# Cross attention of a four-layer decoder: queries masked at the eviction, and the attends of two chunks of heads issued together

## The chip, the cores and the metric

The kernel runs on one core of a Trainium2 chip. A core has a matrix engine (TensorE, in the profile PE, with its weight loads as PEld), a vector engine (VectorE, DVE), a scalar engine (ScalarE, ACT), GpSimd (POOL) and a queue for transfers (SyncE, SP). Each engine works through its own instructions in order, and semaphores tie them together. Matrix products land in PSUM, a small memory of eight banks; DVE or ACT must evict them to the working memory (SBUF). The metric is the device time of one execution in microseconds (us), and the times given are medians of several runs.

## The reference

The model is a decoder of four layers (L0 to L3), each with a self-attention, a cross-attention and a feed-forward part, on 8 sequences of 112 tokens with 256 features; the cross attentions look at 8 contexts of 375 positions with 128 features. Three of the four cross attentions run through the function that is changed here. The one of the last layer stands for them:

```python
Q = (x @ Wq.T).reshape(B, xN, NUM_HEADS, HEAD_DIM)          # 16 heads of 16
KV = (z @ Wkv.T).reshape(B, zN, 2, NUM_HEADS, HEAD_DIM)
attn = jnp.einsum('bqhd,bkhd->bhqk', Q, K) * SCALE          # SCALE = 16 ** -0.5
attn = jax.nn.softmax(attn, axis=-1)
O = jnp.einsum('bhqk,bkhd->bqhd', attn, V).reshape(B, xN, DIM)
return O @ Wo.T
```

That of layer 1 has the same shape and biases on queries, keys, values and output. That of layer 2 (called a2 here, the second of two attentions in its part) has 16 heads of 32 features and no such biases.

## The kernel before

`cross` (from L1260) computes one cross attention. `l1_xattn` calls it for layer 1 (named l1x, with heads of 16), `a2_attend` for layer 2 (a2, heads of 32) and `l3_xattn` for layer 3 (l3x, heads of 16). The heads of 16 are the dense case (`dense = hd == 16`).

The 16 heads are taken as four chunks c of four heads j. One step is a pair (b, c) of a batch b and a chunk c, so a stage has 32 steps. For one step:

- `score(b, c)`: for each of four heads a product of 32 rows on TensorE, queries by keys, into one of four PSUM buffers `sc` of 112 tokens by 375 positions. The four heads lie in four groups of 32 rows of the matrix engine and run side by side.
- `exponent(b, c)`: for each head the maximum over the positions on DVE (L1338, tile `xnm`), then the exponential on ACT (L1342 in the dense case, L1344 in a2, where it also gathers the sum), tile `xe`.
- `turn(b, c, j)`: three transposes on TensorE (L1351) that bring the positions onto the partitions, into one of two PSUM buffers `tr`, and one eviction to the tile `xeT`: heads 0 and 2 on DVE (L1359), heads 1 and 3 on ACT (L1357).
- `attend(b, c)`: the weights by the values, 12 products of 32 columns each (four heads by three pieces of 125 positions, L1367), gathered in the one PSUM buffer `av` of the batch. After the last chunk ACT copies `av` to the tile `xoT` (L1377).

The profile counts two records for each product of 32-bit numbers, one for each transpose, so an attend is 24 records and a step's scores are 8.

Around these stand `key` and `value` (keys and values of the next batch), `query` (queries, by halves of four batches; half 0 ahead of the loop, half 1 within it), `summed` and `divide` (sums of the weights, their reciprocals, and the division) and `result` (the output projection, and its addition to the stream). Keys, values, queries, sums and results all pass through one PSUM buffer, `mm` (the pool `ps1` has one buffer for each name), so whoever writes it next waits until it has been evicted.

In the dense case a row group of 32 rows holds two heads of 16 in the keys. The weights of the queries are laid out by `_halves` (512 columns, half of them zero), so that the query tile `qT` has four chunks in each of which only one of the two heads of a row group is not zero. `score` takes chunk c of `qT` with chunk c // 2 of the keys.

The loop over the steps runs with a schedule written out by hand (L1414): TensorE, DVE and ACT take their instructions in the order of the code. In one step n = (b, c): `turn` of heads 0 and 1; a key chunk of the next batch, or at odd c in the dense case `summed` (c=1) or `divide` (c=3) of the batch before; `turn` of head 2; `score` of step n+1; `turn` of head 3; `exponent` of step n+1; `value` of the next batch (c < 3); at c=3 of the first two batches two chunks of `query` for half 1; at c=3 `result` of the batch before; `attend` of step n. What stands ahead of the loop is ordered by the scheduler of the language.

Steps with c=0 and c=2 are called even below, those with c=1 and c=3 odd.

The weights are packed on the host into blobs, which SyncE loads in order through a ring of eight buffers (`w<-in_w`, and `w<-in_wl` for the last layer). Small columns (biases, scales) lie in one tile, `vec`.

Of the kernel before, what the change touches and what calls it, by code (L numbers as in the profile page):

```python
# [26 lines left out]
AF = mybir.ActivationFunctionType  # L27
ALU = mybir.AluOpType
# [4 lines left out]
P = 128  # L33
# [13 lines left out]
def _fm(w):  # L47

    k, n = w.shape
    return w.reshape(k // P, P, n).transpose(1, 0, 2).reshape(P, -1)  # L50


def _col(v):

    return v.reshape(-1, P).T
# [17 lines left out]
_SLOTS = [8 * (n // 2) + 2 * j + n % 2 for n in range(4) for j in range(4)]  # L73
# [4 lines left out]
    return w.reshape(-1, 16, 16)[:, _SLOTS].reshape(w.shape)  # L78


def _halves(w):

    out = np.zeros((w.shape[0], 4, 4, 2, 16), w.dtype)
    a = w.reshape(-1, 16, 16)[:, _SLOTS].reshape(-1, 4, 4, 16)
    for n in range(4):
        out[:, n, :, n % 2] = a[:, n]
    return out.reshape(-1, 512)

_SHIFT = np.tile(np.arange(32) == 16, 16).astype(np.float32)
# [33 lines left out]
def _weights(inp):  # L125
    def g(layer):
        return lambda name: inp[f"{layer}_{name}"]

    a, xa, f = g("L0_attn"), g("L0_xattn"), g("L0_ffn")
# [33 lines left out]
    a, xa, f = g("L1_attn"), g("L1_xattn"), g("L1_ffn")  # L163
# [9 lines left out]
            ("l1a_bo", _row(a("bo"))),  # L173
        ],
        [
            ("l1x_wq", _fm(_halves(xa("Wq")))),
            ("l1x_wk", xa("Wk")),
            ("l1x_wv", _slots(xa("Wv"))),
            ("l1x_bv", _row(_slots(xa("bv")[None])[0])),
# [7 lines left out]
    for j in range(3):  # L187
        cols = slice(512 * j, 512 * j + 512)
        blobs.append([(f"l1f_gate{j}", _fm(gate[:, cols])), (f"l1f_up{j}", _fm(up[:, cols]))])
    for j in range(2):  # L190
# [1 line left out]
    v1 = [  # L192
        ("l1a_bq", _col(_spread(a("bq")[None])[0])),
        ("l1a_bk", _col(_spread(a("bk")[None])[0] + _SHIFT)),
        ("l1x_bq", _col(_halves(xa("bq")[None])[0])),
        ("l1x_bk", _col(xa("bk"))),
    ]

    a, xa, f = g("L2_attn"), g("L2_xattn"), g("L2_ffn")
# [39 lines left out]
    for pf in ("a1", "a2"):  # L239
        for n in ("lnx_g", "lnx_b", "lny_g", "lny_b", "ln3_g", "ln3_b", "li2_b"):  # L240
            v2.append((f"{pf}_{n}", _col(xa(f"{pf}_{n}"))))

    a, xa, f = g("L3_attn"), g("L3_xattn"), g("L3_ffn")
# [7 lines left out]
    ]  # L251
    last = [
        [
            ("l3x_wq", _fm(_halves(xa("Wq").T))),
            ("l3x_wk", wkv[:, :D]),
            ("l3x_wv", _slots(wkv[:, D:])),
        ],
# [5 lines left out]
    v3 = [  # L263
        ("l3f_s_in", np.broadcast_to(f("s_in")[None, :], (P, 1))),
        ("l3f_s_in_down", np.broadcast_to(f("s_in_down")[None, :], (P, 1))),
    ]
    return (blobs, ternary, last), own, ints, raw, v0 + v1 + v2 + v3


# [110 lines left out]
class _Kernel:  # L380
# [879 lines left out]
    def cross(self, name, cT, qsrc, wq, wk, wv, wo, hd, scale, finish, ctx, bq=None, bk=None, bv=None):  # L1260
# [14 lines left out]
        nc, tc = self.nc, self.tc  # L1275
# [37 lines left out]
        def query(half, c):  # L1313
            cols = slice(half * HT, (half + 1) * HT)
            pm = self.t(ps1, [P, 512], "mm")[:, :HT]
            self.mm(pm, [(wq[:, k, c * P : (c + 1) * P], self.xnT[:, k, cols]) for k in range(2)])
            if bq is None and half == 0:
                nc.scalar.activation(qT[:, c, cols], pm, AF.Copy, scale=scale)
            elif bq is None:
                nc.vector.tensor_scalar(qT[:, c, cols], pm, scale, None, ALU.mult)  # L1320
            else:
                nc.vector.tensor_scalar(qT[:, c, cols], pm, self.v(bq, c), scale, ALU.add, ALU.mult)
# [39 lines left out]
        def attend(b, c):  # L1362
            if c == 0:
                avs[b] = self.t(ps1, [P, 512], "av")
            for i in range(NCH):
                for j in range(4):
                    nc.tensor.matmul(  # L1367
                        avs[b][32 * j : 32 * j + 32, c * S : (c + 1) * S],
                        values[b % 2][:CH, i, 4 * c + j, :],
                        eTs[b, c, j][:, i, :],  # L1370
                        start=i == 0,
                        stop=i == NCH - 1,
                        skip_group_check=True,
                    )
            if c == 3:
                oTs[b] = self.t(work, [P, 4, S], "xoT")
                nc.scalar.copy(oTs[b], avs.pop(b)[:, : 4 * S].rearrange("p (c s) -> p c s", c=4))  # L1377
# [29 lines left out]
        for i in range(NCH):  # L1407
            value(0, i)
        qsrc(ps, 0)
        for c in range(4):  # L1410
            query(0, c)
        qsrc(ps, 1)
        steps = [(b, c) for b in range(NB) for c in range(4)]
        with tc.manual_schedule(engines={ET.PE, ET.DVE, ET.Activation}):  # L1414
            score(0, 0)
            exponent(0, 0)
            for n, (b, c) in enumerate(steps):
                turn(b, c, 0)
                turn(b, c, 1)

                if not dense or c % 2 == 0:
                    if b + 1 < NB:
                        key(b + 1, c * nk // 4)
                elif b > 0:
                    (summed, divide)[c // 2](b - 1)
                turn(b, c, 2)
                if n + 1 < len(steps):
                    score(*steps[n + 1])
                turn(b, c, 3)
                if n + 1 < len(steps):  # L1430
                    exponent(*steps[n + 1])
                if c < 3 and b + 1 < NB:
                    value(b + 1, c)
                if c == 3 and b < 2:
                    query(1, 2 * b)
                    query(1, 2 * b + 1)
                if not dense and b > 0 and c == 1:
                    divide(b - 1)
                if b > 0 and c == 3:
                    result(b - 1)  # L1440
                attend(b, c)
                if not dense and c == 3:
                    summed(b)
            if dense:
                summed(NB - 1)
            divide(NB - 1)
            result(NB - 1)
# [1230 lines left out]
```

## Time and profile before

| | |
|---|---|
| median of 3 runs | 2171.72 us (2168.49 to 2174.79) |
| the profiled execution | 2168.82 us, its span 2167.0 us |
| stage l1x, 706 to 900 | 194 us, PE busy 179.82, DVE 129.57, ACT 100.13 |
| stage a2, 1370 to 1570 | 200 us, PE busy 186.44, DVE 137.16, ACT 121.71 |
| stage l3x, 1871 to 2057 | 186 us, PE busy 173.78, DVE 124.03, ACT 101.60 |
| one full batch, l1x (772.59 to 792.08) | 19.49 us |
| one full batch, a2 (1462.26 to 1482.83) | 20.57 us |
| one query chunk on PE | 1.70 us |
| one attend, start to start of what follows | 0.71 to 0.90 us |
| granted TensorE clock, mean of the span | 0.946 of full speed |

The rows shown further on come from three kinds of view. The page gives the busy time of each engine. A timeline gives, for each merged group of instructions, its start, its duration, the engine, the line of the kernel, the operation, the tile written and those read, the shape of the output and the inputs, the count, and in square brackets the idle time of that engine before it with what ended it. The view of busy time by stretch gives for each stretch its length, then busy time and instruction count of PE, PEld, DVE, ACT and POOL, then the granted clock, the share of the transfer engines and their GB/s. A busy PE is not a PE at its peak: matmuls overlap in its pipeline.

### The profile page before, as it was taken

How to read it: one execution, taken by the hardware profiler on the slowest of the kernel's cores; microseconds unless marked ns; L12 is line 12 of the kernel's file. 1: busy time of each engine (PE TensorE's matmuls, PEld its weight loads, DVE VectorE, ACT ScalarE, POOL GpSimd, SP SyncE). 2: the span in 40 equal slices, each digit the busy share in tenths (PEclk: the TensorE clock that was granted, in tenths of full speed). 3: DMA queues.
4: the chain of work that ended last, by engine and by line, in shares of the span. 5: the costliest groups of instructions: out<-in, count | busy, mean ns of one | idle time of the engine just before them, and what ended most of it. 6: DMA issues, size and time to landing. Idle time of an engine off the chain costs nothing. (4 is left out here: it accounts for less than half of the span.)

```text
span 2167.0 us, 45439 instructions
## 1 busy us (share of the span) xinstructions
PE 1938.5 (89%) x17912; PEld 1244.4 (57%) x17912; DVE 1386.8 (64%) x3905; ACT 869.0 (40%) x2420; POOL 281.9 (13%) x480
## 2 busy tenths in 40 slices
PE   7999999898898899899899989899998997899844
PEld 3545544465666566545566455556667886566623
DVE  5666666686655677553566676567624866667688
ACT  2444444562212456452033223466525322356532
POOL 1111111001302100000001342100003530100000
PEclk9999999998899999999999999999999997999956
DMA  5000001103000000223101010000022210000000
GB/s 208 3 3 3 3 22 39 33 21 107 1 1 16 21 2 2 79 89 135 40 1 59 1 42 8 1 2 2 1 78 72 98 39 26 1 2 2 2 0 17
DMA packets 11486, 69.20 MB, mean 32 GB/s; under 512 B 1290, under 2 KB 3082, under 8 KB 4874
## 3 DMA queue, kind: packets, MB, share of 16 engines
q1 hardware_dynamic: 9684, 54.69, 7.0%
q0 software_dynamic: 1584, 11.54, 1.5%
q8 instruction: 145, 2.38, 0.4%
q14 instruction: 73, 0.60, 0.1%
HBM read 65.30 MB, written 0.92 MB: 31 GB/s over the span
## 5 line engine op out<-in xcount | busy, mean ns | idle before, releaser
L727 PE MATMUL g<-w,hT 128*32 128x256 f32 x3552 | 236.7, 384 | 1.8 <-DVE hT L757 1.5
L1338 DVE TENSOR_REDUCE xnm<-sc 112x1 f32<-112x375 f32 x384 | 184.6, 541 | 40.0 <-PE sc L444 39.4
L1351 PEld LDWEIGHTS tr<-cst,xe 112*125 112x125 f32 x1152 | 151.5, 188 | 94.6 <-issue 38.1
L1351 PE MATMUL tr<-cst,xe 112*125 112x112 f32 x1152 | 192.9, 289 | 6.8 <-DVE xeT L1359 4.2
L727 PEld LDWEIGHTS g<-w,hT 128*32 128x32 f32 x3552 | 93.2, 109 | 121.8 <-DVE hT L757 83.0
L1357 ACT COPY xeT<-tr 125x336 f32<-125x336 f32 x192 | 85.4, 445 | 158.1 <-PE tr L1351 158.1
L444 PE MATMUL mm<-xnT,w 128*128 128x448 f32 x316 | 136.0, 572 | 9.4 <-DVE qT L1320 2.9
L1359 DVE COPY xeT<-tr 125x336 f32<-125x336 f32 x192 | 97.3, 507 | 68.6 <-PE tr L1351 61.8
L690 PE MATMUL g<-xw,cst 128*32 128x256 f32 x1792 | 137.9, 379 | 0.0
L1342 ACT ACTIVATE xe<-sc,xnm 112x375 f32<-112x375 f32 x256 | 126.6, 582 | 7.3 <-DVE xnm L1338 7.3
L753 ACT ACTIVATE th<-cell 128x64 f32<-128x64 f32 x224 | 57.5, 257 | 144.3 <-DVE cell L749 141.9
L444 PE MATMUL mm<-w,hT 128*112 128x256 f32 x448 | 103.4, 392 | 0.0
L740 ACT ACTIVATE sg<-g 128x192 f32<-128x192 f32 x224 | 74.1, 331 | 67.3 <-PE g L727 45.6
L444 PEld LDWEIGHTS mm<-xnT,w 128*128 128x128 f32 x316 | 60.0, 200 | 67.9 <-issue 44.2
L576 POOL TENSOR_TENSOR hTlo<-xnT,hThi 128x448 fp32r<-128x448 f32 x60 | 74.9, 1256 | 160.8 <-issue 82.7
L444 PE MATMUL mm<-hThi,w 128*128 128x448 f32 x256 | 95.2, 372 | 0.0
L444 PE MATMUL mm<-hTlo,w 128*128 128x448 f32 x256 | 94.7, 370 | 0.0
L444 PEld LDWEIGHTS mm<-w,hT 128*112 128x112 f32 x448 | 81.7, 184 | 21.7 <-issue 3.5
L758 POOL COPY hs<-hT 128x16 f32<-128x16 f32 x224 | 51.8, 231 | 318.4 <-DVE hT L757 318.4
L755 DVE TENSOR_TENSOR h<-sg,th 128x64 f32<-128x64 f32 x224 | 50.5, 226 | 63.9 <-ACT th L753 63.8
L444 PE MATMUL sc<-xkT,qT 32*112 32x375 f32 x768 | 89.8, 519 | 0.0
L1367 PE MATMUL av<-xeT,xv 125*32 125x112 f32 x2304 | 86.4, 266 | 2.1 <-ACT xeT L1357 2.1
(482 smaller groups left out, 3961.9 us busy)
## 6 DMA issues: line engine op xcount, KB each, us to landing
w<-in_w SPq DMA_DIRECT2D x22, 1024.0 KB, 5.0
t<-in_wt SPq DMA_DIRECT2D x11, 1024.0 KB, 4.9
w<-in_wt POOLq DMA_DIRECT2D x11, 1024.0 KB, 5.4
raw<-in_wq SPq DMA_DIRECT2D x3, 1024.0 KB, 5.2
cx<-in_ctx SPq DMA_DIRECT2D x2, 1500.0 KB
wi<-in_wint SPq DMA_DIRECT2D x3, 768.0 KB, 5.6
w<-in_w SPq DMA_DIRECT2D x2, 896.0 KB, 10.7
w<-in_w SPq DMA_DIRECT2D x2, 768.0 KB, 4.1
```

Source lines behind the costliest of these rows:

```text
L444: self.nc.tensor.matmul(out, lhsT, rhs, start=i == 0, stop=i == len(pairs) - 1)
L576: nc.gpsimd.tensor_tensor(dst[1], src, dst[0].bitcast(F32), ALU.subtract)
L690: nc.tensor.matmul(g[32 * j : 32 * j + 32, :], pick[:, t % 16, :], xw[:, l, t // 16, 256 * j : 256 * j + 256], start=True, stop=t == 0, sk ...
L727: nc.tensor.matmul(g[32 * j : 32 * j + 32, :], hT[l][:, c, :], whh[l][:, c, 256 * j : 256 * j + 256], start=False, stop=c == 1, skip_group ...
L740: nc.scalar.activation(sg[:, :192], g[:, :192], AF.Sigmoid)
L753: nc.scalar.activation(th, cell[l], AF.Tanh)
L1338: nc.vector.tensor_reduce(nm, sc, AX.X, ALU.max, negate=True)
L1342: nc.scalar.activation(e, sc, AF.Exp, bias=nm)
L1351: nc.tensor.transpose(tp[:CH, i * S : (i + 1) * S], e[:, i * CH : (i + 1) * CH], self.ident[:S, :S])
L1357: nc.scalar.copy(eT, src)
L1359: nc.vector.tensor_copy(eT, src)
L1367: nc.tensor.matmul(avs[b][32 * j : 32 * j + 32, c * S : (c + 1) * S], values[b % 2][:CH, i, 4 * c + j, :], eTs[b, c, j][:, i, :], start=i ...
```

## The change

There are two parts.

The queries of the dense case are no longer spread over four half-empty chunks. Their weights have 256 columns, so `query` makes two chunks, and each is evicted twice into `qT`: once multiplied by a column that is 0.25 in the rows of even heads and 0 in those of odd heads, once by the opposite column (`turn0` and `turn1`, two new columns in `vec`; as l1x's query bias shrinks from four columns to two, the tile keeps its width). In l1x both evictions are on DVE, which adds the bias as well; in l3x the first is on DVE and the second on ACT. `qT` holds the same numbers as before, and `score` is unchanged.

The attends of an even and the following odd step are issued together at the end of the odd step. The place of the queries for half 1 moves: in the dense case one of two chunks at c=3 of each of the first two batches, in a2 one of four chunks at c=1 and c=3 of them.

```diff
-def _halves(w):
-
-    out = np.zeros((w.shape[0], 4, 4, 2, 16), w.dtype)
-    a = w.reshape(-1, 16, 16)[:, _SLOTS].reshape(-1, 4, 4, 16)
-    for n in range(4):
-        out[:, n, :, n % 2] = a[:, n]
-    return out.reshape(-1, 512)
-
+_EVEN = [(np.arange(P) // 16 % 2 == p).astype(np.float32)[:, None] for p in range(2)]
...
-            ("l1x_wq", _fm(_halves(xa("Wq")))),
+            ("l1x_wq", _fm(xa("Wq"))),
...
-        ("l1x_bq", _col(_halves(xa("bq")[None])[0])),
+        ("l1x_bq", _col(xa("bq"))),
...
-            ("l3x_wq", _fm(_halves(xa("Wq").T))),
+            ("l3x_wq", _fm(xa("Wq").T)),
...
+    v3 += [(f"turn{p}", np.float32(0.25) * _EVEN[p]) for p in range(2)]
...
             self.mm(pm, [(wq[:, k, c * P : (c + 1) * P], self.xnT[:, k, cols]) for k in range(2)])
-            if bq is None and half == 0:
+            if dense:
+                for p in range(2):
+                    out, even = qT[:, 2 * c + p, cols], self.v(f"turn{p}")
+                    if bq is not None:
+                        nc.vector.tensor_scalar(out, pm, self.v(bq, c), even, ALU.add, ALU.mult)
+                    elif p:
+                        nc.scalar.activation(out, pm, AF.Copy, scale=even)
+                    else:
+                        nc.vector.tensor_scalar(out, pm, even, None, ALU.mult)
+            elif bq is None and half == 0:
...
         qsrc(ps, 0)
-        for c in range(4):
+        for c in range(nk):
             query(0, c)
...
-                if c == 3 and b < 2:
-                    query(1, 2 * b)
-                    query(1, 2 * b + 1)
+                if dense and c == 3 and b < 2:
+                    query(1, b)
+                elif not dense and c % 2 and b < 2:
+                    query(1, 2 * b + c // 2)
                 if not dense and b > 0 and c == 1:
                     divide(b - 1)
                 if b > 0 and c == 3:
                     result(b - 1)
-                attend(b, c)
+                if c % 2:
+                    attend(b, c - 1)
+                    attend(b, c)
```

## The prediction

> **What bounds the kernel now.** I read the page first, then busy time by stretch for the three stages that run `cross`, then the timeline of one steady batch, first of TensorE (PE) alone, then of all engines. The page makes PE the busiest engine:
>
> ```profile
> PE 1938.5 (89%) x17912; PEld 1244.4 (57%) x17912; DVE 1386.8 (64%) x3905; ACT 869.0 (40%) x2420; POOL 281.9 (13%) x480
> ```
>
> The stages take 194 us (l1x, from 706), 200 us (a2, from 1370) and 186 us (l3x, from 1871); PE is busy 93% of each. That is an average over steps with two different limits. All engines, third batch of l1x, tail of step c=0 and head of c=1:
>
> ```profile
> 775.37 1.91 DVE L1338 TENSOR_REDUCE xnm<-sc 112x1 f32<-112x375 f32 x4 [0.37 <-PE sc L444]
> 775.53 0.30 PEld L444 LDWEIGHTS mm<-w,ctxT 128*125 128x125 f32 x2
> 775.63 0.61 PE L444 MATMUL mm<-w,ctxT 128*125 128x256 f32 x2
> 775.88 0.44 ACT L1357 COPY xeT<-tr 125x336 f32<-125x336 f32 x1 [1.13 <-PE tr L1351]
> 776.17 0.73 PEld L1367 LDWEIGHTS av<-xeT,xv 125*32 125x32 f32 x24 [0.33 <-issue]
> 776.17 0.97 PE L1367 MATMUL av<-xeT,xv 125*32 125x112 f32 x24
> 776.22 1.97 ACT L1342 ACTIVATE xe<-sc,xnm 112x375 f32<-112x375 f32 x4
> 777.07 0.73 PEld L1351 LDWEIGHTS tr<-cst,xe 112*125 112x125 f32 x6 [0.17 <-issue]
> 777.07 0.91 PE L1351 MATMUL tr<-cst,xe 112*125 112x112 f32 x6
> 777.20 0.42 DVE L1309 TENSOR_TENSOR xv<-mm,w 125x256 f32<-125x256 f32 x1
> 777.69 0.51 DVE L1359 COPY xeT<-tr 125x336 f32<-125x336 f32 x1
> ```
>
> The scores of the next step started at 774.38. Their first exponential is done at 776.22 + 0.58 = 776.80; the next transposes start at 777.07. So the attend, 0.90 us from 776.17 to 777.07, is what PE does while it would otherwise wait. Behind it one chain runs without a gap: four maxima, value copy (xv), copy of the turned weights (xeT), and only then the third transposes (two PSUM buffers `tr`). The last batch shows that chain alone, having no keys and values to make (l3x, PE alone):
>
> ```profile
> 2032.56 0.90 PE L444 MATMUL sc<-xkT,qT 32*112 32x375 f32 x8
> ...
> 2034.56 0.76 PE L1367 MATMUL av<-xeT,xv 125*32 125x112 f32 x18 [0.26 <-ACT xeT L1357]
> ...
> 2037.20 0.90 PE L444 MATMUL sc<-xkT,qT 32*112 32x375 f32 x8
> ```
>
> Score to score is 4.64 us, exactly that of c=0 in a full batch (774.38 to 779.02), though 0.54 us of PE work (value) is missing. Taking PE work from an even step therefore buys almost nothing; adding it to an odd step, which is full, costs its length.
>
> **Part 1, queries.** Half 1, second batch of l1x, PE alone:
>
> ```profile
> 764.95 1.68 PE L444 MATMUL mm<-xnT,w 128*128 128x448 f32 x4
> 767.41 1.77 PE L444 MATMUL mm<-xnT,w 128*128 128x448 f32 x4 [0.78 <-DVE qT L1322]
> 769.96 1.98 PE L444 MATMUL mm<-w,xoT 128*112 128x256 f32 x8 [0.78 <-DVE qT L1322]
> ```
>
> A chunk is 1.70 us of PE, and whoever takes the single PSUM buffer `mm` next waits 0.72 to 0.78 us for its eviction. The l1x and l3x stages lose 4 of 8 chunks each; evictions stay 8, two to a chunk. An eviction with a pointer scalar took 0.684 us on DVE (L1322), with an immediate 0.625 (L1320), on ACT 0.544 (L1318). No row has two pointers, or ACT with a pointer scale; I take 0.68 and 0.55, and as upper ends 0.9 (the sum of a 0.68 pass and a 0.2 small DVE row) and the 0.653 of another ACT row with a pointer bias (L810).
> - l1x, first batch: two chunks and a gap, 743.13 to 747.29 = 4.16, become 1.70, the attends not needing `mm`: -2.46. Second batch: the result starts at 769.96; now 764.95 + 1.70, then two DVE evictions, about 768.07: -1.89.
> - l3x, first batch 1903.25 to 1907.35 becomes 1.70: -2.40. Second: DVE and ACT evict one each, but ACT first finishes its exponentials (1925.61 + 1.97), so the result moves from 1929.91 to about 1928.17: -1.74.
> - Before the loop, l1x: the order becomes query, two scores, query, two scores, transposes. With evictions at 719.11 to 720.45, scores at 719.86, second query at 720.7, its evictions to 723.85, the last two maxima to 724.9 and the first copy of turned weights to 725.4, the scores of step (0,1) start at 725.9, not 728.63: -2.7. The l3x analog lands at 1885.2, not 1888.76: -3.5.
> - a2 keeps four chunks but spreads them over c=1 and c=3. At c=1 the value has just taken `mm`, and DVE copies it only after its four maxima (about 1404.07, PE done at 1402.85). The query must wait 1.29 us, and both attends are queued behind it on PE. Before: 4.10 + 4.89 = 8.99 us in two batches; after: twice (1.29 + 1.70), 1.70, and 1.70 + 0.72 = 10.1: +1.1.
> Sum -14.7 + 1.1 = -13.6. Two weight loads on SP's queue shrink by 256 KB each; the queue keeps its order, POOL's nothing changes, and DMA is at 0 to 2% share in these stages: 0 (if a load were late the stage's first key would wait for it, and it waits for DVE).
>
> **Part 2, pairs of attends.** PE alone, an attend after a result:
>
> ```profile
> 791.36 0.78 PE L1367 MATMUL av<-xeT,xv 125*32 125x112 f32 x24
> 792.08 0.91 PE L1351 MATMUL tr<-cst,xe 112*125 112x112 f32 x6
> ```
>
> It holds PE 0.72 us. Its six groups of four start 0.1 apart (0.097 from the second on), the last at 791.87, so some 0.14 of the 0.72 is the change to the transposes. A second attend directly behind costs 6 x 0.097 = 0.58 more if its groups run on, 0.72 at worst (as if alone); I take 0.58, the groups being of one form. After a value the attend takes 0.90, because 0.18 is a wait for the fourth copy on ACT; in a pair that wait is gone.
> - Dense stages, by batch. Even steps: transposes start at 776.86, not 777.07, but behind them the value's buffer and the xeT copy hold; c=0 gains 0.09, c=2 gains 0.12 (its divide waits for that copy, before as after). c=1: 0.90 becomes 0.72 + 0.58, +0.40. c=3: +0.58. Sum +0.77, times 7 full batches = 5.4. Last batch +0.25. In one batch the next stage's normalisation stands differently among DVE's maxima (four rows of 0.41 before the copy instead of three): +0.3. Each stage +5.95, both +11.9.
> - a2: no wait on ACT there (attend 0.71). Even steps -0.16 each. c=1 +0.16: the second transposes wait there for the divide anyway (1472.88, where 1472.09 + 0.37 = 1472.46 would do), and 0.42 of the second attend falls into that. c=3 +0.58. Sum +0.42 by 6 = 2.5, first batch (no divide) +0.8, last +0.3, normalisation +0.3: +3.9.
> Unseen are PE's even-step waits. Bounds: an even step can't go below 4.44, the shortest score-to-score step of the last batch, against 4.64, 4.80 and 4.72 now; that is 0.11, 0.24 and 0.12 a step more than I take, 7 us over 22 batches. A second attend at 0.72 in 48 pairs is 6.7 worse. I stay with the replay, nearest to the 4.64 of the last batch.
>
> **Sum.** -13.6 + 11.9 + 3.9 = +2.2 us on the profiled 2168.82 (span 2167.0 and 1.8 around it): 2171.0. The median, 2171.72, lies 2.9 higher: 2174. I count within 0.3% (6.5 us) as no change, about what a measurement of this kernel can tell: 2165.2 to 2178.2.
>
> **Weighed against the skill.** The Trainium skill, "Perfetto Trace Analysis", section on the most-contended engine, says to optimise the busiest engine first. The last batch's 4.64 speaks against it here; by the rule, with PE work setting all steps, the sum would be about 30 us of gain.
>
> One pair of rows warns of the clock (busy time by stretch; the column after POOL's is the granted clock):
>
> ```profile
> 836.00:839.00 3.00, 2.56 (x24) 1.82 (x22) 2.70 (x8) 1.00 (x3) 0.62 (x1) 1.00 0.01 3
> 839.00:843.00 4.00, 4.00 (x38) 2.87 (x35) 2.28 (x6) 2.31 (x5) 0.00 (x0) 0.57 0.00 0
> ```
>
> After 0.44 us of short PE waits the clock fell to half for 3.4 us, and that step took 5.86 instead of 4.48: 1.4 us. The change adds a wait of some 0.7 us to every even step. The last batch of each stage, with 0.6 us of waits in each step, kept 1.00, so I count no more such events. The skill's "TensorE: Matmul & The Clock Gate", section "A second HAM failure mode: psum-queue depth-cycling", says that frequent micro-idles make the clock oscillate; by it every pair could lose 1.4 us, some 60 in all, while no run here shows that.
>
> **Rivals.**
> - *The clock drops (slower).* For: the two rows. Against: the last batches. At 1.4 us an event, four more make it slower by over 0.3%; one in each of 22 batches gives +31, so 2205. Chance 0.10.
> - *Pairing at full price (slower).* Second attend 0.72 and no even step shorter: +6.7 and, for the lost 0.21 (dense) and 0.32 (a2) a batch, +5.4, so +14.3: 2186. Chance 0.12.
> - *The query saving is hidden (doesn't do what it says).* Double evictions hold `mm` longer and DVE's later copies slip; half of 14.7 goes: +9.6, 2181. Against: DVE idles 1.8 to 2.1 us in these steps. Chance 0.06.
> - *PE sets the even step (faster).* For: 89% busy and the 0.90 attend. Against: the 4.64. At the floor of 4.44 it gives 2167, still no change; with both attends' 0.90 (a2 0.71) taken out of every batch's even steps about 2142. It decides where each of the 44 even steps shortens by 0.2 us more than I take. Chance 0.12.
> - My forecast, 0.60; its own range is 2167 to 2181.
>
> **Numbers.** Faster 0.12, same 0.60, slower 0.10 + 0.12 + 0.06 = 0.28. The range 2163 to 2187 takes in both ends of the pairing and the two nearer slow rivals, and leaves out most of the clock's case and half of the fast one.
>
> **What would show it.** PE should wait 0.6 to 0.7 us for ACT's xe before the transposes of odd steps in l1x; score to score should read about 4.55, 4.88, 4.68, 6.15 in a full batch where it was 4.64, 4.48, 4.80, 5.57; two attends together 1.30. Step (0,1)'s scores should come 2.7 (l1x) and 3.5 us (l3x) sooner after the first query; in a2 a query should wait about 1.3 us for the value's copy. Wrong if even steps shorten by over 0.3 us, or the granted clock shows new stretches of 0.50.

## The result, and the profile after

The changed kernel takes 2177.4 us in the median of nine executions (2175.3 to 2190.0), beside 2170.2 us for the kernel before on the same chip: 1.0043 times as long, with a 95% interval from 1.0030 to 1.0055. A second set, given as an experiment below, says 1.0040 (1.0026 to 1.0054). So the change makes the kernel slower, by +7 us between medians and by 9 us by the ratio. I had put 2174.0 us and +2.2 us, and 0.28 on slower. Of all executions below, one of e10 took 2533.08 us at a mean granted clock of 0.723; it is left out of that ratio.

The profiled execution of the changed kernel is the slowest of the nine, at 2189.99 us. Its steady batch on TensorE alone, third batch of l1x (columns as in the timelines of the prediction; L1354 are the transposes, L1370 the attends, L438 the helper of all products):

```profile
772.71 0.90 PE L438 MATMUL sc<-xkT,qT 32*112 32x375 f32 x8
...
774.49 1.36 PE L1370 MATMUL av<-xeT,xv 125*32 125x112 f32 x48
775.78 0.91 PE L1354 MATMUL tr<-cst,xe 112*125 112x112 f32 x6
...
777.58 0.90 PE L438 MATMUL sc<-xkT,qT 32*112 32x375 f32 x8
...
780.05 1.04 PE L1354 MATMUL tr<-cst,xe 112*125 112x112 f32 x6 [0.61 <-ACT xe L1345]
...
782.27 0.90 PE L438 MATMUL sc<-xkT,qT 32*112 32x375 f32 x8
...
785.34 1.36 PE L1370 MATMUL av<-xeT,xv 125*32 125x112 f32 x48
...
788.43 0.90 PE L438 MATMUL sc<-xkT,qT 32*112 32x375 f32 x8
```

From these scores on, score to score reads 4.87, 4.69 and 6.16 us, and 4.58 into the first of them (from 768.13); I had put 4.55, 4.88, 4.68 and 6.15. The two attends hold PE from 774.49 to 775.78, 1.29 us; I had put 1.30. Before the transposes of the odd step PE waits 0.61 us for ACT's `xe`; I had put 0.6 to 0.7. A batch takes 20.30 us instead of 19.49, +0.81 where the prediction said +0.77. The step-by-step replay is right to some hundredths of a microsecond.

What isn't in the replay stands in the last batch of the same stage. TensorE alone, then busy time by stretch (length, then busy time and instruction count of PE, PEld, DVE, ACT and POOL, the granted clock, the share of the transfer engines, GB/s):

```profile
872.08 0.90 PE L438 MATMUL sc<-xkT,qT 32*112 32x375 f32 x8
...
874.55 1.04 PE L1354 MATMUL tr<-cst,xe 112*125 112x112 f32 x6 [1.06 <-ACT xe L1345]
...
876.80 1.61 PE L438 MATMUL sc<-xkT,qT 32*112 32x375 f32 x8
...
879.24 2.47 PE L1370 MATMUL av<-xeT,xv 125*32 125x112 f32 x48
...
883.78 0.90 PE L438 MATMUL sc<-xkT,qT 32*112 32x375 f32 x8
```

```profile
876.50:878.50 2.00, 2.00 (x11) 0.73 (x11) 0.67 (x3) 0.00 (x0) 0.61 (x1) 0.50 0.00 0
878.50:880.50 2.00, 2.00 (x31) 1.80 (x35) 1.91 (x4) 1.10 (x3) 0.00 (x0) 0.50 0.00 0
880.50:882.50 2.00, 2.00 (x32) 1.67 (x25) 0.00 (x0) 1.20 (x3) 0.00 (x0) 0.50 0.00 0
```

The even step has no attend, key or value left here: PE waits 1.06 us for `xe`, until 874.55. By 876.50 the granted clock stands at 0.50. The scores take 1.61 us instead of 0.90, the pair of attends 2.47 instead of 1.36, and the step from 876.80 to 883.78 takes 6.98 us; it took 4.44 before. PE's rows look busy, 2.00 us of 2.00, which is what a half clock looks like in a timeline: no idle time, only longer instructions. The stretch that the kernel before had in the sixth batch of this stage (839 to 843 in the prediction's rows) is there too, from 835.45: its step takes 6.48 us instead of 4.87.

In l3x this execution loses the clock in the middle batches too, in three in a row and then in the last; one of them, by stretch:

```profile
2026.00:2028.00 2.00, 1.77 (x13) 0.83 (x13) 1.23 (x3) 0.70 (x3) 0.00 (x0) 1.00 0.01 4
2028.00:2030.00 2.00, 1.46 (x11) 1.24 (x11) 1.93 (x5) 2.00 (x5) 0.00 (x0) 1.00 0.00 0
2030.00:2032.00 2.00, 2.00 (x13) 1.77 (x16) 0.64 (x2) 0.21 (x1) 0.61 (x1) 0.53 0.03 8
2032.00:2034.00 2.00, 2.00 (x12) 0.95 (x5) 0.92 (x3) 0.00 (x0) 0.00 (x0) 0.50 0.00 0
2034.00:2036.00 2.00, 2.00 (x31) 1.35 (x33) 1.45 (x4) 1.89 (x5) 0.00 (x0) 0.50 0.00 0
```

The 0.77 us wait of PE before `xe` lies between 2027.78 and 2028.55, and the clock falls at 2030. From its first to its last scores l3x takes 172.94 us here. In a second execution of the same kernel (below) it takes 160.72 us, without one such stretch.

### The profile page after: what moved, and what is told of

Same layout as the page of the kernel before. It is cut to its first block, busy times and chain, and to the rows that moved or that the text cites. A ratio compares the mean times of both kernels' runs of the same rounds, so it can differ in the third digit from the quotient of the medians.

```text
span 2188.2 us, 45327 instructions
## 1 busy us (share of the span) xinstructions
PE 1937.3 (89%) x17880; PEld 1251.1 (57%) x17880; DVE 1386.2 (63%) x3905; ACT 869.5 (40%) x2420; POOL 280.3 (13%) x480
## 5 line engine op out<-in xcount | busy, mean ns | idle before, releaser
L1354 PEld LDWEIGHTS tr<-cst,xe 112*125 112x125 f32 x1152 | 160.1, 194 | 143.7 <-ACT xe L1345 39.3
L1354 PE MATMUL tr<-cst,xe 112*125 112x112 f32 x1152 | 207.6, 301 | 32.4 <-ACT xe L1345 22.4
L438 PE MATMUL mm<-xnT,w 128*128 128x448 f32 x284 | 122.7, 576 | 6.4 <-DVE xv L1301 2.4
L438 PE MATMUL mm<-w,hT 128*112 128x256 f32 x448 | 103.0, 391 | 0.0
L438 PE MATMUL mm<-hThi,w 128*128 128x448 f32 x256 | 94.6, 370 | 0.0
L438 PE MATMUL mm<-hTlo,w 128*128 128x448 f32 x256 | 94.2, 368 | 0.0
L438 PEld LDWEIGHTS mm<-w,hT 128*112 128x112 f32 x448 | 81.4, 183 | 21.8 <-issue 3.7
L438 PE MATMUL sc<-xkT,qT 32*112 32x375 f32 x768 | 92.5, 538 | 1.5 <-DVE qT L1319 0.9
L438 PEld LDWEIGHTS mm<-xnT,w 128*128 128x128 f32 x284 | 55.0, 203 | 57.4 <-issue 41.6
L684 PEld LDWEIGHTS g<-xw,cst 128*32 128x32 f32 x1792 | 58.7, 110 | 38.7 <-issue 0.3
```

The lines of the kernel that those rows point to most:

```text
L438: self.nc.tensor.matmul(out, lhsT, rhs, start=i == 0, stop=i == len(pairs) - 1)
L684: nc.tensor.matmul(g[32 * j : 32 * j + 32, :], pick[:, t % 16, :], xw[:, l, t // 16, 256 * j : 256 * j + 256], start=True, stop=t == 0, sk ...
L1354: nc.tensor.transpose(tp[:CH, i * S : (i + 1) * S], e[:, i * CH : (i + 1) * CH], self.ident[:S, :S])
```

## The experiments

Two theories stood against each other. Theory A: the replay is right at an unchanged clock, and the rest is clock lost behind the waits that pairing exposes. Theory B: a pair costs more on the path than I replayed, at full clock. The runs are called e1 to e11, as in what was expected of them.

### The two parts alone

Queries alone (e1): the attends stay one in each step, and a2 keeps its query chunks at c=3.

```diff
-                elif not dense and c % 2 and b < 2:
-                    query(1, 2 * b + c // 2)
...
+                elif not dense and c == 3 and b < 2:
+                    query(1, 2 * b)
+                    query(1, 2 * b + 1)
...
-                if c % 2:
-                    attend(b, c - 1)
-                    attend(b, c)
+                attend(b, c)
```

> The query part of the change alone, dense stages; each step keeps its own attend, and a2's queries stay two chunks at c=3. The replay of the prediction says -14.7 us (l1x -7.05, l3x -7.64) against the kernel before, about 2155 to 2156, with the half-clock stretches of the kernel before and no new ones, since no PE wait of over 0.3 us is added in a steady step. The rival 'the query saving is hidden' says about half of it: -7, 2163.

Measured: 2158.58 us, 0.9934 (0.9916 to 0.9953), so -12.8 us between medians and -14.3 by the ratio. From the first key product to the last projection l1x takes 182.60 us instead of 189.60, -7.00, and l3x 176.37 instead of 183.79, -7.42; the replay had -7.05 and -7.64. What did differ by a little was the evictions: with two pointers DVE takes 0.739 us (I took 0.68), ACT with a pointer scale 0.638 (I took 0.55). The query saving isn't hidden: the product it takes away is gone, and the pair of evictions is what the result then waits for, 1.49 us (TensorE alone, second batch of l1x):

```profile
765.18 1.68 PE L438 MATMUL mm<-xnT,w 128*128 128x448 f32 x4
768.36 1.98 PE L438 MATMUL mm<-w,xoT 128*112 128x256 f32 x8 [1.49 <-DVE qT L1315]
```

Pairs alone (e2): the kernel before, with only this changed.

```diff
-                attend(b, c)
+                if c % 2:
+                    attend(b, c - 1)
+                    attend(b, c)
```

> The pairing alone, with the queries of the kernel before. The replay says +11.9 in the dense stages and +3.9 in a2 at an unchanged clock: +15.8, about 2186. Theory A (the waits of 0.6 us that pairing leaves in front of the transposes of odd steps let the granted clock fall to half) says more than that and unevenly: +18 to +35, 2188 to 2205, with new stretches of 0.50 in the steady batches of at least one stage, and runs that differ by 10 us and follow the mean granted clock. Theory B (the pair is dearer on the path than I replayed, at full clock) says the same total without new stretches, and score to score of a steady batch more than 0.8 us longer than before at a clock of 1.00.

Measured: 2195.17 us, 1.0102 (1.0081 to 1.0123), +23.8 us between medians and +22 by the ratio; the replay said +15.8. A steady dense batch is 20.30 us and one of a2 21.08, as in the changed kernel. Beside that the trace has half-clock stretches in the last batches of all three stages, in l1x's sixth batch (as in the kernel before) and in two middle batches of l3x (6.48 and 7.65 us for steps of 4.87). This is what theory A asks for.

### The waits filled

The next runs leave the schedule of the changed kernel alone and give PE something useless to do in the wait. What is added writes 64 columns of the bank of `av` that nothing reads (e3).

```diff
+        def filler(b, c):
+            if c == 0:
+                avs[b] = self.t(ps1, [P, 512], "av")
+            for g in range(8):
+                for j in range(4):
+                    nc.tensor.matmul(
+                        avs[b][32 * j : 32 * j + 32, 448:512],
+                        values[b % 2][:CH, g % NCH, 4 * c + j, :],
+                        self.ident[:CH, :64],
...
                 if c % 2:
                     attend(b, c - 1)
                     attend(b, c)
+                else:
+                    filler(b, c)
```

> The changed kernel with 8 groups of four useless matmuls (32 x 64, tiled as an attend is, into 64 columns of the bank of av that nothing reads) where an even step no longer has an attend: between the value and the next transposes. By their shape between 0.33 and 0.8 us of PE, most of it inside the wait of 0.61. Theory A: the path is unchanged (0 to +0.1 us in each of 48 even steps, 0 to +5), but the clock keeps to 1.00 in the steady batches; so all runs lie near the best of the changed kernel, 2171 to 2177, within 4 us of each other, and l3x's batches take 20.3 us each without a stretch of 0.50. Theory B: 0 to +5 on the changed kernel's median of 2177, 2177 to 2182. A third view, that the clock falls because of load and not of waits, says more and longer stretches of 0.50 than in the changed kernel, over 2182.

Measured: 2183.61 us, 1.0053 (1.0034 to 1.0072). The time was a miss, and a plain one: the filler's groups start 0.112 us apart at 64 columns, those of an attend 0.096 at 112, so the filler held PE 1.03 us and did not fit the wait. A steady dense batch became 20.70 us instead of 20.30, one of a2 21.91 instead of 21.08. From first to last scores that is 11.0 us in the three stages: 163.05 in l1x and 163.34 in l3x against 160.12 and 160.69 in e7 below, 178.81 in a2 against 173.40 in the changed kernel. Its clock is another matter: no stretch at 0.50 stands inside any of the three stages' loops, the mean granted clock is 0.947, and the six executions lie within 5 us (2181.3 to 2186.1).

The changed kernel again (e5):

> The changed kernel itself, beside the next runs. Both theories: 2175 to 2190, most runs near 2177. Theory A (clock), sharpened by the traces so far: in the last batch of l1x and of l3x PE waits 1.06 us after each even step, and the granted clock falls to 0.50 right behind the first of these waits, in this execution too, so that the steps of c=1 and c=2 there take 11.5 to 11.8 us together (9.1 in the kernel before).

Measured: 2177.84 us, 1.0040 (1.0026 to 1.0054); c=1 and c=2 of l1x's last batch take 11.95 us together (6.13 and 5.82), as expected; those of l3x 9.00, not as expected: there the clock falls behind the second wait of 1.06 us, after the last scores, and the last projection starts 14.14 us behind these (12.85 in e3). Most useful in this trace is a2's last batch (TensorE alone, then by stretch):

```profile
1563.17 0.90 PE L438 MATMUL sc<-xkT,qT 32*112 32x375 f32 x8
...
1565.72 3.02 PE L1354 MATMUL tr<-cst,xe 112*125 112x112 f32 x12 [1.15 <-ACT xe L1347]
1568.54 2.51 PE L438 MATMUL mm<-w,xoT 128*112 128x256 f32 x8
...
1574.33 1.98 PE L438 MATMUL mm<-w,xoT 128*112 128x256 f32 x8 [0.79 <-DVE xoT L1403]
```

```profile
1561.40:1564.80 3.40, 2.95 (x24) 1.89 (x20) 2.10 (x5) 1.73 (x7) 0.00 (x0) 1.00 0.00 0
1564.80:1568.20 3.40, 2.48 (x11) 2.18 (x12) 1.93 (x5) 2.92 (x10) 0.00 (x0) 0.73 0.02 5
1568.20:1571.60 3.40, 3.40 (x38) 2.61 (x41) 0.79 (x4) 0.44 (x1) 0.01 (x1) 0.77 0.00 0
```

A wait of 1.15 us, then 3.02 us for twelve transposes. From the last scores to the last projection a2 takes 11.16 us here and 10.12 without pairs (e1).

The filler in the last batches of the dense stages alone (e6):

```diff
-                else:
+                elif dense and b == NB - 1:
                     filler(b, c)
```

> The changed kernel with the 8 groups of useless matmuls only in the last batch of l1x and of l3x, four places in all, where the wait is 1.06 us and the filler 1.13. Theory A: the last batches keep the clock at 1.00 and take 9.0 instead of 11.6 us over those two steps, so -2.6 in each stage, -5 on the changed kernel of the same call, about 2172; the run-to-run spread, which comes from the middle batches, stays. Theory B (the pair's own length): 0 to +0.4.

Measured: 2178.47 us, 1.0038 (1.0024 to 1.0053): no gain, where I had put -5. The trace shows that the cause was met and the gain was not kept. The last batch of l1x, TensorE alone and by stretch:

```profile
871.52 0.90 PE L438 MATMUL sc<-xkT,qT 32*112 32x375 f32 x8
...
872.86 1.10 PE L1370 MATMUL av<-cst,xv 125*32 125x64 f32 x64
873.99 1.04 PE L1354 MATMUL tr<-cst,xe 112*125 112x112 f32 x6
...
876.08 0.90 PE L438 MATMUL sc<-xkT,qT 32*112 32x375 f32 x8
...
877.42 1.42 PE L1384 MATMUL av<-xeT,xv 125*32 125x112 f32 x48
...
880.51 0.90 PE L438 MATMUL sc<-xkT,qT 32*112 32x375 f32 x8
```

```profile
873.00:875.00 2.00, 1.97 (x72) 1.75 (x68) 1.81 (x5) 1.98 (x5) 0.00 (x0) 1.00 0.01 4
875.00:877.00 2.00, 2.00 (x21) 1.35 (x19) 0.88 (x3) 0.66 (x2) 0.62 (x1) 1.00 0.00 0
877.00:879.00 2.00, 2.00 (x53) 1.72 (x54) 1.91 (x4) 1.42 (x4) 0.00 (x0) 1.00 0.00 0
```

The clock holds, the pair takes 1.42 us, the two steps 4.56 and 4.43, and the whole stage 186.47 us instead of 190.63. But the clock falls at 894, in the passage to the next stage, and stays at half until 908, where the changed kernel (e5) had 3.4 us of it. The gap from l1x's last scores to a2's first grew from 506.85 to 509.76 us, in code that is the same in both but for the last filler.

The same places filled with eight transposes instead (e7):

```diff
-            for g in range(8):
-                for j in range(4):
-                    nc.tensor.matmul(
...
+            for _ in range(8):
+                nc.tensor.transpose(avs[b][:CH, 448:512], self.ident[:64, :CH], self.ident[:64, :64])
```

> As the run before, but the filler is eight transposes (64 x 125 to 125 x 64, about 1.0 to 1.2 us of PE by the 0.15 us that one of 112 x 125 takes) instead of matmuls. If any busy PE holds the clock, it equals the run with matmuls, 2172. If transposes do not count towards the clock as matmuls do, the last batches fall to 0.50 as in the changed kernel: 2177.

Measured: 2173.86 us, 1.0021 (1.0005 to 1.0037), in two clusters (2166.8 to 2170.2 and 2177.5 to 2182.8, six executions each). The interval overlaps that of the run before, so nothing follows from the two times. The trace says more: l1x's last batch keeps the clock at 1.00, its steps take 4.56 and 4.44, the stage 186.45 us. The Trainium skill, "TensorE: Matmul & The Clock Gate", section "Part 4: PE-mode transpose", says that transposes don't count as PE activity in the way matmuls do; in l1x's last batch 1.08 us of 32-bit transposes held the clock just as 1.10 us of matmuls did. It is one trace of each, and in l3x's last batch e7 loses the clock at 2042.84, behind the last scores, where the fillers of matmuls (e3, e6, e9) kept it. So e7 contradicts the sentence in l1x and doesn't settle it.

Then matmuls cut to the wait, in every even step of the dense stages (e9):

```diff
-            for g in range(8):
+            for g in range(7 if b == NB - 1 else 4):
...
-                else:
+                elif dense:
                     filler(b, c)
```

> The changed kernel with useless matmuls in the even steps of l1x and l3x only, cut to the wait: 4 groups (a group took 0.14 us in e3, so 0.56 for a wait of 0.61), 7 groups (0.99 for 1.06) in the last batches. Theory A: in some executions of the paired kernels the clock falls once a batch in l3x (first to last scores 172.9 and 172.6 us in two traces, 160.7 in three others), and the last batches of l1x and l3x fall too; the filler stops that and the path stays as it is (20.3 us a dense batch, l3x 160.7, at most 161.5). So 2170 to 2176 in the median, a spread of at most 6 us, none over 2180, mean clock 0.946 or 0.947 where the changed kernel has 0.944. If the clock is not set by these waits: median 2177 to 2180 and runs up to 2185 as before.

Measured: 2173.05 us, 1.0006 (0.9991 to 1.0021). The median is where theory A put it, below the changed kernel by 5 us and clear of its interval by the ratios (up to 1.0021 against 1.0026 and more), with the steady dense batch at 20.30 us as in the changed kernel. The spread is not: 2165.1 to 2178.5, with a mean clock from 0.949 to 0.942. The dense stages of the profiled execution have no stretch at 0.50 inside their loops, and this execution is the fastest of the twelve; I have no trace of a slow one.

### a2's part

The dense stages changed, a2 not (e10):

```diff
-                if c % 2:
+                if not dense:
+                    attend(b, c)
+                elif c % 2:
                     attend(b, c - 1)
                     attend(b, c)
```

and a2's two query chunks back at c=3, as in e1.

> The change in l1x and l3x alone; a2 keeps one attend in each step and its two query chunks at c=3. My replay gave a2 +5.0 (queries +1.1, pairs +3.9); the stage totals of the traces so far (first key to last projection 204.0 in the changed kernel, 197.5 with the queries alone) say +6.5. So 2171 to 2173, that is 5 to 6.5 below the changed kernel's 2178, with the same spread of 10 us or more from the clock in the paired stages. If a2's part were nothing, 2178.

Measured: 2170.94 us, 1.0000 (0.9987 to 1.0014). So a2's part of the change costs 6.9 us against the 2177.84 above (by the two ratios 8.7), and the dense part, saved queries against pairs, comes to nothing. The wait that the prediction put in front of a2's query is there in the changed kernel, 1.20 us for the value's copy, with both attends behind it (trace of e5, TensorE alone):

```profile
1403.05 1.03 PE L438 MATMUL mm<-w,yT 128*125 128x512 f32 x2
1405.29 1.77 PE L438 MATMUL mm<-xnT,w 128*128 128x448 f32 x4 [1.20 <-DVE xv L1301]
1406.99 1.36 PE L1370 MATMUL av<-xeT,xv 125*32 125x112 f32 x48
```

### One attend in each step, but a step late

Since a pair leaves one step without an attend, I tried the opposite: an attend in each step, that of the step before, whose turned weights are long there (e4, from e1).

```diff
-                attend(b, c)
-                if not dense and c == 3:
-                    summed(b)
-            if dense:
-                summed(NB - 1)
+                if n > 0:
+                    attend(*steps[n - 1])
+                if not dense and c == 0 and b > 0:
+                    summed(b - 1)
+            attend(*steps[-1])
+            summed(NB - 1)
```

> The queries of e1, one attend in each step, but that of the step before (its weights were all turned a step ago, so PE has not to wait 0.18 us for ACT's fourth copy before it); the sums and the division of a batch stay where they are in the dense stages and move one step later in a2. The replay says that even steps gain 0.09 and 0.12, c=1 0.18, a batch 0.39, so -5.5 over fourteen full dense batches, and +0.7 for the last attend of each of three stages: -3 on e1, about 2152. If the attend's place is worth nothing because DVE's chain sets the even steps altogether, e4 equals e1 within 2 us; if the later copy of av now holds up the sums, it is some 0.5 us a batch slower, +10 on e1. Clock as in e1.

Measured: 2188.45 us, 1.0080 (1.0055 to 1.0104), +30 on the queries alone where I had put -3. The cause is in one row of PE, in the first step of l1x's third batch:

```profile
771.01 0.61 PE L438 MATMUL mm<-w,ctxT 128*125 128x256 f32 x2
772.98 0.78 PE L1370 MATMUL av<-xeT,xv 125*32 125x112 f32 x24 [1.36 <-DVE xv L1303]
```

The late attend of c=3 stands behind the next batch's first value, and the two buffers of values are used in turn: that value goes into the buffer which the attend still has to read. So PE waits for DVE's copy, once in six batches of each stage (1.36 us in a steady batch of l1x; the 18 waits are 26.0 us together), and the attend reads one piece of the wrong batch. The next run (e8), in the dense stages only and with the sums moved out of the way, has the same fault.

```diff
-                if not dense or c % 2 == 0:
+                if not dense or c < 2:
                     if b + 1 < NB:
-                        key(b + 1, c * nk // 4)
+                        key(b + 1, c)
                 elif b > 0:
-                    (summed, divide)[c // 2](b - 1)
+                    (summed, divide)[c - 2](b - 1)
...
-                attend(b, c)
+                if not dense:
+                    attend(b, c)
+                elif n > 0:
+                    attend(*steps[n - 1])
...
             if dense:
+                attend(*steps[-1])
```

> The queries alone (e1), with the attends one step late in the dense stages only, and there the sums moved from c=1 to c=2 and the division from c=2's tail to c=3, the second key chunk taking the place at c=1, so that the late copy of av is not waited for. e4's steps with that wait (5.95 and 5.99) left out read 4.43, 4.70 and 5.58 in a dense batch; with 4.6 for the fourth a batch is 19.3 against 19.49 in e1: -0.18 times 14, -2.6, and +1 for the two last attends: about -1.5 on e1's 2158.6. If the division then holds up the result at c=3, 0 to +10.

Measured: 2166.96 us, 0.9990 (0.9980 to 1.0000), 5.73 us where 4.6 was expected, once a batch. Neither run says anything of late attends. They do say something of the clock. In e8's l1x PE waits six times, 1.36 to 1.90 us, and the clock holds throughout; the longest of these waits, TensorE alone and then by stretch:

```profile
836.50 0.78 PE L1370 MATMUL av<-xeT,xv 125*32 125x112 f32 x24 [1.90 <-DVE xv L1303]
```

```profile
834.00:836.50 2.50, 0.60 (x4) 0.19 (x2) 2.50 (x10) 2.25 (x5) 0.00 (x0) 1.00 0.00 0
836.50:839.00 2.50, 2.50 (x35) 1.94 (x35) 1.42 (x4) 1.22 (x4) 0.00 (x0) 1.00 0.00 0
```

Of the 30 waits of this kind in e4 and e8 (1.20 to 2.39 us), four were followed by a stretch at 0.50 within 2.3 us. So a long wait alone does not bring the clock down.

A third buffer of values in the dense stages mends the fault (e11):

```diff
-        values = [self.t(acts, [P, NCH, 16, 32], f"xv{i}") for i in range(2)]
+        values = [self.t(acts, [P, NCH, 16, 32], f"xv{i}") for i in range(3 if hd == 16 else 2)]
...
-            src, dst = pm.rearrange("p (h d) -> p h d", h=16), values[b % 2][:CH, i, :, :hd]
+            src, dst = pm.rearrange("p (h d) -> p h d", h=16), values[b % len(values)][:CH, i, :, :hd]
...
-                        values[b % 2][:CH, i, 4 * c + j, :],
+                        values[b % len(values)][:CH, i, 4 * c + j, :],
```

> As the run with late attends in the dense stages, with three buffers of values instead of two there: with two, the attend of c=3, being issued behind the next batch's first value, read that value in the first of its three pieces (the wait of 1.36 us for DVE's xv in e4, and 5.73 instead of 4.64 in each batch). So those two runs changed the computation in that piece, and this one doesn't. Without that wait a dense batch should be 4.6 + 4.58 + 4.70 + 5.58 = 19.46 against 19.49 for the queries alone: no gain, 2157 to 2160. By the earlier count of 0.06 to 0.1 a step with 4.43 for the step that took 4.58 it is 19.3, -2.6 in all: 2155 to 2157. If the sums or the division are held up instead, over 2162.

Measured: 2152.91 us, 0.9907 (0.9891 to 0.9924), the best of all kernels here, 17.8 us below the kernel before as measured beside it; its six executions lie within 2.8 us (2150.5 to 2153.2). The intervals of e1 and e11 overlap by a little (0.9916 to 0.9924). A steady step, TensorE alone:

```profile
774.46 0.90 PE L438 MATMUL sc<-xkT,qT 32*112 32x375 f32 x8
775.29 0.58 PE L1354 MATMUL tr<-cst,xe 112*125 112x112 f32 x3
775.70 0.61 PE L438 MATMUL mm<-w,ctxT 128*125 128x256 f32 x2
776.24 0.78 PE L1370 MATMUL av<-xeT,xv 125*32 125x112 f32 x24
776.96 1.02 PE L1354 MATMUL tr<-cst,xe 112*125 112x112 f32 x6
777.81 0.88 PE L438 MATMUL mm<-cst,xoT 128*112 128x4 f32 x8
...
779.04 0.90 PE L438 MATMUL sc<-xkT,qT 32*112 32x375 f32 x8
```

PE waits for nothing from scores to scores in this step; in the whole batch it waits once, 0.28 us. The step takes 4.58 us and the batch 19.27 (4.41, 4.58, 4.70, 5.58) against 19.49. The four steps together gain 0.22 us, 3.1 in fourteen batches, and less than the 0.39 I had first counted. From first to last scores l1x and l3x are together 4.85 us shorter than in e1 (153.04 and 153.23 against 156.21 and 154.91), of which 1.38 is the half-clock stretch in l1x's sixth batch that e1 has and e11 has not. No stretch at 0.50 lies between the first and the last scores of l1x or of l3x.

## Why the prediction was right or wrong

The time lay in the range. The median, 2177.4 us, is just inside the band that the prediction counted as no change (up to 2178.2); the ratio, 1.0043, is just outside its 0.3%. So the likeliest case was missed by little, and the kernel is slower by 0.4%. The table sets the prediction's steps against the traces, each from the first key product to the last projection of a stage, with the half-clock stretches taken out (the stretch of 1.38 us in l1x before, 5.86 instead of 4.48; the changed side from the filled runs e6, e7 and e9, whose full dense batches are those of the changed kernel).

| step | predicted | measured at full clock |
|---|---|---|
| queries, l1x and l3x | -7.05 and -7.64 | -7.00 and -7.42 |
| l1x with pairs | -1.1 | -1.75 (186.47 against 189.60 - 1.38) |
| l3x with pairs | -1.7 | -1.3 (182.50 against 183.79: 8.96 to the first scores and 160.69 to the last in e7, 12.85 behind them in e3) |
| a2, both parts | +5.0 | +5.6 (173.40 against 167.81 from scores to scores) |
| sum | +2.2 | +2.5 |

- *What bounds the kernel.* Right. Taking 0.90 us of attend out of a dense even step shortened it by 0.06 to 0.11 us; the second attend in an odd step cost its length, 0.58 us.
- *Queries.* Right to 0.3 us over both stages. The evictions are 0.06 and 0.09 us longer than taken, which came to little.
- *Pairs.* Right: +0.81 for +0.77 in a dense batch, +0.51 for +0.42 in a2, 1.29 us for 1.30.
- *a2.* The queries' wait of 1.20 us for the value's copy is there. From scores to scores a2 takes 172.45 us with the pairs alone (e2), so the pairs cost 4.6 us where I had 3.9, and the queries 0.95 where I had 1.1.
- *The clock.* This step failed. The prediction had it as "The last batch of each stage, with 0.6 us of waits in each step, kept 1.00, so I count no more such events". Two things were wrong in it. It took the last batches of the kernel before as proof for those after, though the change lengthens just these: 0.26 and 0.36 us in two pieces before, one wait of 1.06 (a2 1.15) beside 0.23 to 0.37 after. And it treated an event that had happened once as one that a few clean batches exclude. In the traces of the kernels with pairs and no filler there, the clock fell behind at least one of the two long waits of the last batch in four of four in l1x, six of six in a2 and four of four in l3x; filled, in none of four in l1x and not in the one of a2, while in l3x one of four (e7, the transposes) still lost it just behind the last scores. The price is 2.7 to 3.0 us in l1x (c=1 and c=2 together against the 8.99 of e6), 1.0 in most of a2's and 1.3 to 5.3 in l3x (to the last projection, against 182.50 in all), not the 1.4 us that I took from the one event of the trace before. The prediction's own sign of being wrong, new stretches of 0.50, is what came.
- *The middle batches.* Their wait of 0.61 us cost the clock in l3x in two of six traces without a filler, and in none of the four others: about 9.5 us in three batches of the first trace of the changed kernel, 4.4 us in two of e2. (The 172.6 us of e2's l3x don't stand against 160.7, as I took them in what I expected of e9: e2 has the queries of the kernel before, which cost 5.95 us more there, 160.86 in the kernel before against 154.91 in e1.) In l1x the sixth batch lost 1.6 us in three of the six (the first trace of the changed kernel, e2, e10), but there the kernel before and e1, with an attend in each step, lose 1.4 too, so it doesn't take pairs. In the traces with a filler, e3 and e9, no middle batch lost it. So the "clock drops" rival was right in its mechanism, at a chance that I had set at 0.10, and its extreme, an event in each batch, did come, in the last four batches of one stage of one execution. The filler cut to the wait brought the median back to the kernel before's, 1.0006, near the +2.5 us of the table.

What else a wait needs to bring the clock down stays open. Its length does not decide: the waits of e4 and e8 were longer and mostly harmless, and the 1.45 to 1.49 us for which the first result behind the new queries waits, twice in each of the eleven traces with these queries, was never followed by a stretch at 0.50. Nor does PE's busy share. In all thirteen traces every half-clock stretch starts on one grid of 3.413 us, by the trace's record of the granted clock, and lasts a whole number of its steps; but within the three stages the clock fell behind grid steps in which PE was busy 30 to 92%, and held behind many of 56 to 70%. Where the grid lies against the loop differs from execution to execution, which can be why the same wait costs the clock in one and not in another. The losses in a row fit that: three of l3x's stretches in the first trace start at 1982.32, 2006.22 and 2030.11, seven grid steps apart, and the batches with them take 23.5 to 24.3 us, about as long. This is argued, not shown.

So of the 7 us (by the ratio 9), 2.5 are the change's own sum, and the traces put the rest on the clock: in the second trace of the changed kernel l1x is 4.2 us longer than with its last batch filled, a2's end 1.0 us and l3x 1.3 us, against the one event of 1.4 us in the kernel before, so +5.1 us net. That it is the waits and not the pairs is shown for the last batches of l1x and a2, where filling the wait removed the stretch in every trace. For the middle batches it is only made likely: two traces of l3x with a filler there are clean, and so are four of the six without.

The other rivals fell. "Pairing at full price" needed a second attend of 0.72 us; it took 0.58. "The query saving is hidden" needed half of 14.7 to go; the queries alone gave 12.8 to 14.3. "PE sets the even step" needed 0.2 us an even step more; the shortest steady one went from 4.64 to 4.58.

What stays open too is the clock between the stages. When the last batches of l1x and l3x were filled, the median did not move with matmuls (e6) and fell by 4 us with transposes (e7), with overlapping intervals. In e6's trace a stretch of 13.6 us stands behind l1x in place of the 3.4 of the unfilled ones, in e3's one of 6.8, in those of e7 and e9 none. From l1x's last scores to a2's first the traces read 501.5 to 510.2 us, in code of which the change touches only the ends, and the executions of the kernel before alone run from 2166.6 to 2179.3 us. Whether a stretch that is kept out of a stage makes one behind it likelier can't be told from one trace of each kernel.

The prediction also weighed a rule of the Trainium skill, "TensorE: Matmul & The Clock Gate", section "A second HAM failure mode: psum-queue depth-cycling": frequent micro-idles make the clock oscillate. It was set aside in favour of a row of the trace, and it describes what came, in a milder form: by an event in every pair it would have been some 60 us, while the runs show about 5 us in the typical execution and some 13 more in the slowest of nine (2189.99 against the median).

## What to carry to other kernels

Work that fills a wait is not free to move, even when the path doesn't need it there: read the granted clock behind every wait that the edit opens, above all in the last rounds of a loop, where the other filler work has already run out. An attend in each step, but a step late, left PE no wait of more than 0.28 us in a steady batch and gave the fastest kernel here, once its buffers were deep enough. And when work is moved behind a write into a rotating buffer, count the buffers again: a sudden wait for that write on the moved instruction is the sign that it reads the wrong round.

## What the runs showed that I had not expected

- In each of 14 last batches at least one of two waits of 1.06 to 1.15 us was followed by 3.4 or 6.8 us at half clock. Waits of 0.61 to 0.77 us did the same in l3x in some executions, batch after batch, and not in others, while 22 waits of 1.45 to 1.49 us elsewhere in the same stages never did.
- Groups of four filler matmuls of 64 columns started 0.112 us apart, those of an attend's, of 112 columns, 0.096. Fewer columns did not make the groups shorter; the two differ in their operands as well.
- Executions of one kernel differ by more than the change does: 2166.6 to 2179.3 us for the kernel before, the slowest four at mean clocks of 0.941 and 0.942, the fastest at 0.947 and 0.948. The kernel with late attends, whose steady batches have one PE wait of 0.28 us, stayed within 2.8 us in six.
